# Decoder layer in fp32 on one core: self-attention's v copied by quarters of the rows instead of by copies, with other places for gated transfers and for the closing loads

## The chip, the cores and the metric

The kernel runs on one core of one Trainium2 chip. A core has a matrix engine (TensorE, PE in the profile; PEld is its weight load), a vector engine (DVE), a scalar engine (ACT), GpSimd (POOL) and a queue for transfers (SP). Each takes its instructions in the order of the program and waits for the others through semaphores. SP and ACT both issue DMA transfers: those of SP are queue q1 of the profile, those of ACT are q10. The metric is the device time of one execution in microseconds (us). The kernel before took 848.33, 846.91 and 843.43 us in three runs, median 846.91.

## The reference

One post-norm decoder layer on x (2 x 1024 x 256) with a context of 77 rows per batch entry, all in float32:

```
def _L0_attn_ref(x, Wq, Wk, Wv, Wo, bo):          # 16 heads of 64
    q, k, v = split_heads(x @ Wq), split_heads(x @ Wk), split_heads(x @ Wv)
    q, k = apply_rope(q), apply_rope(k)
    sim = einsum('bid,bjd->bij', q, k) * scale
    sim = where(causal, sim, -inf)
    out = einsum('bij,bjd->bid', softmax(sim), v)
    return merge_heads(out) @ Wo + bo

x = layernorm(x + _L0_attn_ref(x, ...))
x = layernorm(x + _L0_xattn_ref(x, ctx_1024, ...))  # 16 heads over 77 keys
x = layernorm(x + _L0_ffn_ref(x, ...))              # upper half of the rows by w_r through gelu(x W1 + b1) W2 + b2
```

The change is in the first of the three, self-attention, which ends at about 550 us of the 843 us.

## The kernel before

Self-attention works on 16 pairs of heads (2 batch entries x 8), `Pair` n = 0 to 15. Its steps have letters, and the order of all instructions is written out by hand in lists of them: `opening` (L526), a list `steps` (L487) that is run once per period with an offset of pairs for each step, and `ending` (L539). `("V6", -1)` in period p does step V6 of pair p - 1. The order holds for every engine: each gets its part of the list in this order.

The steps of a pair, with the engine that does them:

- `L`: loads its columns of Wk, Wq, Wv (three transfers on SP, w_pair). `Pk`, `Pq`, `Pv`: projections (PE), `E`: their copies out of PSUM (ACT). Digits after them are halves of the 1024 rows.
- `d`: a transfer that swaps neighbouring rows of k and q (turned<-raw, two on SP). `c`, `s`, `a`: the rotation by cosine and sine, on POOL. A half of k and q is ready after its `a`.
- `w` (`spread`, L314): stores v (128 partitions x 1024 numbers) in DRAM as v_d, four quarters of 32 rows. `l` (`copies`, L318): loads v_d back four times into the tile v4, issued by ACT: each group of 32 partitions gets all of v. There is one v4 (`bufs=1`).
- `S0` to `S4`: scores of five groups of query tiles (PE); `T`: mask and row maxima (DVE); `X`: exponentials (ACT); `R`: transposes by 32 x 32 blocks (DVE).
- `V0` to `V7` (`output`, L399): the product of the probabilities with v. Because the transposes are by blocks of 32, the matmuls have 32 rows, and each of the four row groups of PE reads its own copy in v4: matmul (k, j, r) of Vn reads `v4[rows of r, 8k + n, half j]`. These are 488 short matmuls per pair (7808 in all, L410).
- `O`: copies the output out of PSUM (ACT, `gathered`). `Q`, `I`: the row sums turned into a row and inverted; `D`: stores the inverse in DRAM (inv_d); `B` (`along`, L390): loads it back over 64 partitions twice (over<-inv_d, SP). `M` (`scaled`, L430): out times over, on POOL. `W`: stores the pair's result (attn_d).

The closings (`Closing`, L438) make an output tile of 128 rows from all eight pairs: `A` (first batch entry) and `f` (second) load attn_d, `C`/`F` project, `Y`/`g` and `Z`/`z` normalise.

Almost all transfers of SP go through `begin` (L217). It knows a `gate`: after V1 of a pair, `output` puts its last matmul there, and the next transfer that `begin` issues waits for that matmul. What stands behind it on SP waits too.

`pieces` (L228) says for each pair how many extra splits its score and projection matmuls get (`split`), so that the same columns are done in more and smaller instructions.

In the periods in the middle, PE does, from V7 of one pair to V0 of the next: scores, projections for later pairs, scores; then V0 and V1, scores, V2 to V4, scores, V5, V6, V7. `l` for the next pair's V stands behind V7, since v4 is then free.

Of the kernel before, what the change touches and what calls it, by code (L numbers as in the profile page):

```python
# [16 lines left out]
P, R32 = 128, 32  # L17
B, T, C = 2, 1024, 256
# [4 lines left out]
NT = T // P  # L23
# [11 lines left out]
def decoder_layer(  # L35
# [104 lines left out]
    keys = [(b, hp) for b in range(B) for hp in range(NP)]  # L140
# [5 lines left out]
    with (  # L146
# [78 lines left out]

        pieces = [0, 2, 12, 13, 11, 10, 11, 12, 13, 11, 8, 9, 8, 8, 9, 0]  # L228
        left = [pieces[0]]

        def split(first, last, most):
# [14 lines left out]
        class Pair:  # L246
# [71 lines left out]
            def copies(self):  # L318

                self.v4 = s1.tile([P, K4, P], F32, tag="v4", name="v4")  # L320
                for r in range(4):
                    nc.scalar.dma_start(
                        self.v4[r * R32 : (r + 1) * R32, :, :].rearrange("k (c n) d -> k c (n d)", c=4),
                        self.v_d.rearrange("c k e -> k c e"),
                    )


# [71 lines left out]
            def output(self, n):  # L399
                if n == 0:  # L400
                    self.po = [ring.tile([P, NT, R32], F32, tag="t", name="po_self") for _ in range(4)]
                for k in range(4):
                    for j in range(2):
                        first = (NT * n + n, NT * (n + 1) + n)[j]
                        step = (1, NT)[j]
                        last = first + (NT - 1 - n) * step + 1

                        for r in range(k if n == NT - 1 else 0, 4):
                            rows = slice(r * R32, (r + 1) * R32)
                            ins = TE.matmul(  # L410
                                self.po[r][j * D : (j + 1) * D, n:, :],
                                self.v4[rows, NT * k + n, j * D : (j + 1) * D],
                                p_t[rows, first:last:step, k * R32 : (k + 1) * R32],
                                start=(n == 0 and k == 0), stop=(n == NT - 1 and k == r),
                            )
                if n == 1 and self.n < len(keys) - 1:
                    gate[:] = [ins]

            def gathered(self, r):
# [18 lines left out]
        class Closing:  # L438
# [47 lines left out]

        steps = [  # L487
# [40 lines left out]
            0Ev4 0T01 1Pq1 0X00 0c1 0s1 0X01 1Eq1 1Ek1 1Pv0 0a1 0S1 2L 0R00 0w 0R01 1d1 1Pv4 1c1 1Pq0 0T10 0T11  # L528
            0S2 1Ev4 0T21 0X10 1Ev0 1Eq0 1Pk0 1s1 1w 0X11 2Pq1 0T20 0l 0R10 1Ek0 1d0 0S3 0R11 0X21 0X20 0T30
            2Pk0 1a1 0T31 0X30 1c0 0S4 0X31 0R20 1s0 0R30 0R21 1a0 2Eq1 0T40 3L 2Pv4 0T41 2Pv0 0X40 0X41 2Ek0  # L530
            0R31 0R40 2Pq0 2Ev4 5= 1S0 0R41 1T00 2Eq0 2Ev0 0V0 1T01 0V1 2w 0V2 1S1 1T11 0V3 1X00 2d0 0V4 0V5 1T10
            1S2 1X01 1X11 1R00 0V6 0V7 1X10 0O0 1T20 1T21 1S3 1R10 1R01 0O1 2c0 1l 1X20 1T31 2Pk1 0O3 1T30 0O2
            3Pv4 0Q 2Ek1 1S4 2c1 1X30 2s0 1X21 3Pq1 1R20 3Ev4 3Pv0 2a0 1R11 3Pk0 0I 1T41 2d1 1R30 1X31 3Pq0 1T40
            2S0 1R21 1X41 1X40 1R31 1R40 0D 1R41 2T00 3Ek0 2s1 3Eq1 4L 2a1 3Eq0 3Ev0 1V0 1V1 0B 2T01 2X00 1V2 2S1
            1V3 1V4 2T10 2T11 1V5 2R00 2S2 2X01 2T20 2T21 1V6 2X11 2R01 1V7 3d0 3c0
        """


        ending = """  # L539
            14S3 14R11 15s0 14X20 12M 14R20 14X10 14X21 14R10 13O0 14l 13O1 14R21 14T31 15Pk1 15a0 13Q 14T30 13I  # L540
            14S4 14X31 14X30 13O2 14R31 14T41 14X41 14T40 14R30 14R41 4C 12W 13D 15Ek1 15d1 5A 15c1 4Y 13O3 14X40 14R40
            15S0 15s1 15T01 15a1 14V0 15T00 15X01 14V1 13B 14V2 15S1 14V3 14V4 15T10 15T11 15X00 14V5
            15R00 15X11 15S2 14V6 14V7 15X10 15T20 15T21 14O0 15R01 15S3 14O3 5C 15R10 15l 15X21 13M 15T30 15X20
            15T31 15R11 15R21 15X30 15R20 15X31 15R30 14O1 13W 15S4 14Q 15T41 15T40 5U 15R31 14I 14O2 15X41
            15X40 6A 6C 1= 15R40 15R41 15Q 15I 5Y 6U 0f 1f 1= 15V0 14D 4Z 14B 6Y 15V1 15V2 15V3 7A 15V4 5Z 14M 15V5 7C 0n 15V6
            6Z 15D 15B 15V7 15O3 15O0 15O1 2f 15O2 0F 1F 0g 2F 0z 1g 1z 7U 2g 3f 2z 3F 3g 7Y 3z 4f 4F
            4g 7Z 5f 6f 7f 0N 1N 5F 6F 5g 6g 7F 4z 7g 5z 6z 7z
        """
# [569 lines left out]
```

## Time and profile before

| | |
|---|---|
| three runs | 848.33, 846.91, 843.43 us |
| profiled execution | 844.46 us, span 842.7 us |
| mean granted clock of TensorE | 0.983 |
| v<-v_d, issued by ACT | 64 transfers of 512 KB |
| turned<-raw, SP | 64 of 256 KB, 4.3 us from issue to landing (median) |
| v_d<-v, SP | 16 of 512 KB, 4.5 us |
| over<-inv_d, SP | 32 of 256 KB, 4.2 us |
| attn_d<-out_pair, SP | 14 of 512 KB, 3.9 us |
| instruction reads (q8) | 90 packets, 1.47 MB |

The profile is one execution. Its groups of instructions have columns "line, engine, operation, out<-in, form, count | busy us, mean ns of one | idle us of the engine just before them and what ended most of it"; "issue" is idle time in which the engine waited for nothing that the profile shows. A row of the timeline begins with start and length in us. A table by stages has PE, PEld, DVE, ACT and POOL busy times with counts, then the granted clock, the share of the 16 DMA engines' time, and GB/s. Queue rows have packets, MB and the share of 16 DMA engines' span that the packets took. The trace also holds each DMA packet with its queue, size, start and length; a transfer's completion is one packet of 4 bytes from each DMA engine that it used.

### The profile page before, as it was taken

How to read it: one execution, taken by the hardware profiler on the slowest of the kernel's cores; microseconds unless marked ns; L12 is line 12 of the kernel's file. 1: busy time of each engine (PE TensorE's matmuls, PEld its weight loads, DVE VectorE, ACT ScalarE, POOL GpSimd, SP SyncE). 2: the span in 40 equal slices, each digit the busy share in tenths (PEclk: the TensorE clock that was granted, in tenths of full speed). 3: DMA queues.
4: the chain of work that ended last, by engine and by line, in shares of the span. 5: the costliest groups of instructions: out<-in, count | busy, mean ns of one | idle time of the engine just before them, and what ended most of it. 6: DMA issues, size and time to landing. Idle time of an engine off the chain costs nothing.

```text
span 842.7 us, 26522 instructions
## 1 busy us (share of the span) xinstructions
PE 794.6 (94%) x11432; PEld 628.9 (75%) x11432; DVE 575.5 (68%) x1306; ACT 358.2 (43%) x845; POOL 364.4 (43%) x261
## 2 busy tenths in 40 slices
PE   8999999999999999999999999899999999999886
PEld 5566688788788788787788777688778887776645
DVE  2658679668668668678768778345677788866664
ACT  2545456555456555455454455002433333233120
POOL 2633554554454555365463641222133322440473
PEclk9999999999999999999999999899999999999988
DMA  5445377477467577667467476661360000110130
GB/s 187 148 137 140 108 203 199 155 192 203 123 174 193 161 209 197 170 174 188 143 167 190 140 177 174 174 215 44 102 240 1 1 1 1 42 60 1 51 112 38
DMA packets 65329, 112.32 MB, mean 133 GB/s; under 512 B 6498, under 2 KB 43708, under 8 KB 65212
## 3 DMA queue, kind: packets, MB, share of 16 engines
q1 hardware_dynamic: 54459, 72.87, 26.8%
q10 hardware_dynamic: 9216, 33.56, 18.3%
q0 software_dynamic: 1536, 4.20, 1.3%
q8 instruction: 90, 1.47, 0.7%
q14 instruction: 28, 0.22, 0.1%
HBM read 71.24 MB, written 22.59 MB: 111 GB/s over the span
## 4 chain that ended last, share of the span: by engine, by line
PE 84%; DVE 9%; issue 4%; POOL 1%; ACT 1%; DMA 0%; POOLq 0%; SPq 0%; DVEq 0%; ACTq 0%
PE po_self L410 18%; PE ps_scores L342 16%; PE pp_kq L268 13%; PE pp_v L303 7%; PE ps_cross L934 6%; PE po_cross L977 6%; PE po_proj L473 5%; PE po_ffn L886 3%; PE pp_h L875 3%; DVE reach L800 2%; DVE pT L372 2%; PE unread L244 1%; DVE p L355 1%; PE pt_p L965 1%; DVE e L943 1%
## 5 line engine op out<-in xcount | busy, mean ns | idle before, releaser
L355 DVE CUSTOM_DVE_ANT_0 p<-ps_scores,fence 128x512 f32<-128x512 f32 (+7 forms) x256 | 179.7, 751 | 124.1 <-PE ps_scores L342 123.6
L363 ACT ACTIVATE p<-p,neg 128x768 f32<-128x768 f32 (+7 forms) x256 | 196.3, 768 | 160.2 <-DVE neg L355 158.3
L410 PE MATMUL po_self<-pT,v 32*64 32x256 f32 (+6 forms) x7808 | 160.5, 300 | 22.2 <-issue 18.6
L372 DVE STREAM_TRANSPOSE pT<-p 128x768 f32<-128x768 f32 (+7 forms) x256 | 175.7, 740 | 4.1 <-ACT p L363 2.5
L410 PEld LDWEIGHTS po_self<-pT,v 32*64 32x64 f32 x7808 | 139.6, 134 | 47.1 <-issue 35.0
L342 PE MATMUL ps_scores<-kq 64*128 64x256 f32 (+3 forms) x1056 | 150.6, 417 | 1.8 <-issue 1.5
L342 PEld LDWEIGHTS ps_scores<-kq 64*128 64x128 f32 x1056 | 94.4, 189 | 43.5 <-issue 29.9
L268 PE MATMUL pp_kq<-xT,w_pair 128*128 128x256 f32 (+2 forms) x516 | 118.8, 383 | 0.8 <-ACT xT L203 0.8
L288 POOL TENSOR_TENSOR kq<-raw,cos 128x1024 f32<-128x1024 f32 x31 | 73.2, 2362 | 105.9 <-ACT raw L276 105.9
L291 POOL TENSOR_TENSOR turned<-turned,sin 128x1024 f32<-128x1024 f32 x31 | 73.2, 2362 | 103.2 <-DMA turned<-raw 103.2
L268 PEld LDWEIGHTS pp_kq<-xT,w_pair 128*128 128x128 f32 x516 | 87.2, 191 | 24.7 <-issue 11.6
L955 POOL TENSOR_TENSOR e<-e,inv 128x616 f32<-128x616 f32 x32 | 38.2, 1217 | 116.6 <-DVE inv L954 83.4
L120 POOL TENSOR_TENSOR rs<-ve,neg_half 128x1 f32<-128x1 f32 x48 | 27.4, 576 | 116.4 <-DVE ve L118 114.2
L295 POOL TENSOR_TENSOR kq<-kq,turned 128x1024 f32<-128x1024 f32 x31 | 73.5, 2370 | 1.4
L977 PE MATMUL po_cross<-packed,pT 128*128 128x256 f32 (+1 forms) x320 | 71.8, 379 | 0.1
L934 PE MATMUL ps_cross<-wqk,x1T 128*128 128x308 f32 x256 | 69.3, 424 | 1.4 <-ACT x1T L924 1.4
L977 PEld LDWEIGHTS po_cross<-packed,pT 128*128 128x128 f32 (+1 forms) x320 | 60.8, 190 | 10.2 <-issue 0.5
L303 PEld LDWEIGHTS pp_v<-w_pair,xT 128*128 128x128 f32 x512 | 61.1, 192 | 4.0 <-issue 2.2
L303 PE MATMUL pp_v<-w_pair,xT 128*128 128x128 f32 x512 | 62.2, 275 | 0.0
L934 PEld LDWEIGHTS ps_cross<-wqk,x1T 128*128 128x128 f32 x256 | 47.4, 190 | 17.9 <-ACT x1T L924 1.7
L947 ACT ACTIVATE e<-e 128x616 f32<-128x616 f32 x32 | 22.9, 717 | 76.7 <-DVE e L943 75.4
L473 PE MATMUL po_proj<-wo,attnT 128*128 128x256 f32 x224 | 51.7, 383 | 0.5 <-DVE out_pair L428 0.5
(123 smaller groups left out, 816.8 us busy)
## 6 DMA issues: line engine op xcount, KB each, us to landing
v<-v_d ACTq DMA_DIRECT2D x64, 512.0 KB, 8.3
turned<-raw SPq DMA_DIRECT2D x64, 256.0 KB, 4.3
v_d<-v SPq DMA_DIRECT2D x16, 512.0 KB, 4.5
over<-inv_d SPq DMA_DIRECT2D x32, 256.0 KB, 4.2
attn_d<-out_pair SPq DMA_DIRECT2D x14, 512.0 KB, 3.9
attnT<-attn_d SPq DMA_DIRECT2D x8, 512.0 KB, 5.5
vo_d<-vo SPq DMA_DIRECT2D x2, 1232.0 KB
attnT<-attn_d SPq DMA_DIRECT2D x3, 768.0 KB, 5.4
```

The source lines that it names most:

```text
L268: TE.matmul(pp[:, cols], self.w[:, c, "kq".index(of), :], x_ts[self.b, n][:, c, cols], start=(c == 0), stop=(c == NC - 1),)
L288: E.tensor_tensor(self.kq[:, :, n * NB : (n + 1) * NB], self.raw[n], self.twice(cos, n), ALU.mult)
L295: E.tensor_tensor(dst, dst, self.turned[n], ALU.add)
L303: TE.matmul(pv[:, i, :], x_ts[self.b, 2 * n // NT][:, c, toks], self.w[:, c, 2, :], start=(c == 0), stop=(c == NC - 1),)
L342: TE.matmul(self.ps[j][:, cols], self.kq[rows, 1, t * P : (t + 1) * P], self.kq[rows, 0, cols.start - at : cols.stop - at], start=True, st ...
L355: V.tensor_tensor_reduce(p[:, span], self.ps[j][:, span], fence[:, T - (t + 1) * P :], -SCALE, -MASKED, ALU.add, ALU.min, neg[:, i : i + 1],)
L363: A.activation(p[:, span], p[:, span], AF.Exp, bias=neg[:, i : i + 1], scale=-1.0, accum_out=self.sums[:, j, t : t + 1],)
L372: V.transpose(p_t[:, first : first + t * step + 1 : step, :], self.p[g, j][:, span].rearrange("p (n k) -> p n k", k=P),)
L410: ins = TE.matmul(self.po[r][j * D : (j + 1) * D, n:, :], self.v4[rows, NT * k + n, j * D : (j + 1) * D], p_t[rows, first:last:step, k * R ...
L473: TE.matmul(self.po, of, wo[:, c, :], start=(c == 0), stop=(c == NP - 1))
L934: TE.matmul(ps[:, g, : Q * S], self.x_t[:, c, :], wqk[:, c, self.b, h : h + Q, :].rearrange("p h s -> p (h s)"), start=(c == 0), stop=(c = ...
L977: TE.matmul(po, self.p_t[:w, k, :], packed[self.b][:w, k, :], start=(k == 0), stop=(k == NK - 1))
```

## The change

It has four parts.

1. **copies.** Four transfers of 512 KB remain. Each brought all of v to one group of 32 partitions; now each brings one quarter of the rows (32 rows of 4 KB) to all four groups, 128 partitions, by a source that repeats the quarter four times.
2. **Gates and places.** `output` sets the gate after V6 as well as after V1. `w` moves from between V1 and V2 to behind V6, and `B` from the same place to behind `w` (in the opening: 2w behind 0V6, 0B behind 1V6; there d of the next pair takes the gate of V1).
3. **pieces.** Five of the sixteen entries grow by one; their sum goes from 137 to 142.
4. **Ending.** The load 5A moves from before V0 of pair 14 to behind its V1, 13B from behind V1 to behind V6 of pair 14, 6A from before V0 of pair 15 to behind 13B, and 0f and 1f from before V0 of pair 15 to behind its V3 and the load 7A.

```
-        pieces = [0, 2, 12, 13, 11, 10, 11, 12, 13, 11, 8, 9, 8, 8, 9, 0]
+        pieces = [0, 2, 13, 13, 12, 10, 11, 13, 13, 12, 8, 9, 8, 9, 9, 0]
...
-                for r in range(4):
+                for c in range(4):
                     nc.scalar.dma_start(
-                        self.v4[r * R32 : (r + 1) * R32, :, :].rearrange("k (c n) d -> k c (n d)", c=4),
-                        self.v_d.rearrange("c k e -> k c e"),
+                        self.v4[:, c * NT : (c + 1) * NT, :].rearrange("p n d -> p (n d)"),
+                        self.v_d[c].unsqueeze(0).to_broadcast([4, R32, NT * P]),
                     )
...
-                if n == 1 and self.n < len(keys) - 1:
+                if n in (1, NT - 2) and self.n < len(keys) - 1:
                     gate[:] = [ins]
...
-            ("T00", 0), ("T01", 0), ("s1", 0), ("V0", -1), ("a1", 0), ("V1", -1), ("d0", 1), ("B", -2), ("w", 1), ("S1", 0), ("V2", -1),
+            ("T00", 0), ("T01", 0), ("s1", 0), ("V0", -1), ("a1", 0), ("V1", -1), ("d0", 1), ("S1", 0), ("V2", -1),
...
-            ("V6", -1), ("T21", 0), ("V7", -1), ("X10", 0), ("X20", 0), ("O1", -1), ("S3", 0),
+            ("V6", -1), ("w", 1), ("B", -2), ("T21", 0), ("V7", -1), ("X10", 0), ("X20", 0), ("O1", -1), ("S3", 0),
...
-            14S4 14X31 14X30 13O2 14R31 14T41 14X41 14T40 14R30 14R41 4C 12W 13D 15Ek1 15d1 5A 15c1 4Y 13O3 14X40 14R40
-            15S0 15s1 15T01 15a1 14V0 15T00 15X01 14V1 13B 14V2 15S1 14V3 14V4 15T10 15T11 15X00 14V5
-            15R00 15X11 15S2 14V6 14V7 15X10 15T20 15T21 14O0 15R01 15S3 14O3 5C 15R10 15l 15X21 13M 15T30 15X20
+            14S4 14X31 14X30 13O2 14R31 14T41 14X41 14T40 14R30 14R41 4C 12W 13D 15Ek1 15d1 15c1 4Y 13O3 14X40 14R40
+            15S0 15s1 15T01 15a1 14V0 15T00 15X01 14V1 5A 14V2 15S1 14V3 14V4 15T10 15T11 15X00 14V5
+            15R00 15X11 15S2 14V6 13B 6A 14V7 15X10 15T20 15T21 14O0 15R01 15S3 14O3 5C 15R10 15l 15X21 13M 15T30 15X20
...
-            15X40 6A 6C 1= 15R40 15R41 15Q 15I 5Y 6U 0f 1f 1= 15V0 14D 4Z 14B 6Y 15V1 15V2 15V3 7A 15V4 5Z 14M 15V5 7C 0n 15V6
+            15X40 6C 1= 15R40 15R41 15Q 15I 5Y 6U 1= 15V0 14D 4Z 14B 6Y 15V1 15V2 15V3 7A 0f 1f 15V4 5Z 14M 15V5 7C 0n 15V6
```

More of the change, by code (lines that the diff above doesn't have):

```diff
@@ L530, in decoder_layer @@
             2Pk0 1a1 0T31 0X30 1c0 0S4 0X31 0R20 1s0 0R30 0R21 1a0 2Eq1 0T40 3L 2Pv4 0T41 2Pv0 0X40 0X41 2Ek0
-            0R31 0R40 2Pq0 2Ev4 5= 1S0 0R41 1T00 2Eq0 2Ev0 0V0 1T01 0V1 2w 0V2 1S1 1T11 0V3 1X00 2d0 0V4 0V5 1T10
-            1S2 1X01 1X11 1R00 0V6 0V7 1X10 0O0 1T20 1T21 1S3 1R10 1R01 0O1 2c0 1l 1X20 1T31 2Pk1 0O3 1T30 0O2
+            0R31 0R40 2Pq0 2Ev4 5= 1S0 0R41 1T00 2Eq0 2Ev0 0V0 1T01 0V1 2d0 0V2 1S1 1T11 0V3 1X00 0V4 0V5 1T10
+            1S2 1X01 1X11 1R00 0V6 2w 0V7 1X10 0O0 1T20 1T21 1S3 1R10 1R01 0O1 2c0 1l 1X20 1T31 2Pk1 0O3 1T30 0O2
             3Pv4 0Q 2Ek1 1S4 2c1 1X30 2s0 1X21 3Pq1 1R20 3Ev4 3Pv0 2a0 1R11 3Pk0 0I 1T41 2d1 1R30 1X31 3Pq0 1T40
-            2S0 1R21 1X41 1X40 1R31 1R40 0D 1R41 2T00 3Ek0 2s1 3Eq1 4L 2a1 3Eq0 3Ev0 1V0 1V1 0B 2T01 2X00 1V2 2S1
-            1V3 1V4 2T10 2T11 1V5 2R00 2S2 2X01 2T20 2T21 1V6 2X11 2R01 1V7 3d0 3c0
+            2S0 1R21 1X41 1X40 1R31 1R40 0D 1R41 2T00 3Ek0 2s1 3Eq1 4L 2a1 3Eq0 3Ev0 1V0 1V1 3d0 2T01 2X00 1V2 2S1
+            1V3 1V4 2T10 2T11 1V5 2R00 2S2 2X01 2T20 2T21 1V6 0B 2X11 2R01 1V7 3c0
         """
```

## The prediction

> **What bounds the kernel now.** I read the page first: engines, then the queues, then the costliest groups.
>
> ```profile
> span 842.7 us, 26522 instructions
> PE 794.6 (94%) x11432; PEld 628.9 (75%) x11432; DVE 575.5 (68%) x1306; ACT 358.2 (43%) x845; POOL 364.4 (43%) x261
> q1 hardware_dynamic: 54459, 72.87, 26.8%
> q10 hardware_dynamic: 9216, 33.56, 18.3%
> ...
> L410 PE MATMUL po_self<-pT,v 32*64 32x256 f32 (+6 forms) x7808 | 160.5, 300 | 22.2 <-issue 18.6
> ...
> v<-v_d ACTq DMA_DIRECT2D x64, 512.0 KB, 8.3
> ```
>
> TensorE is busy for 94%, so only a new PE wait or a removed one moves the end. The removable one stands in the L410 row: 22.2 us of idle time before the output matmuls, nearly all "issue". The profile's own time is 844.46 us, 1.8 above its span and 2.45 below the median 846.91; I sum against 844.46.
>
> v's copies are all of queue q10 (ACT issues nothing else). To see where they lie I took one pair's stretch in the timeline, the waits on v_d, and the busy table from the copies' issue to V0 of the next pair:
>
> ```profile
> 259.86 0.31 ACTq L322 DMA_DIRECT2D v<-v_d  x1
> ...
> 260.48 1.27 ACTq L322 DMA_DIRECT2D v<-v_d  x3
> ...
> 275.98 3.50 PE L410 MATMUL po_self<-pT,v 32*64 32x256 f32 x128
> ...
> 289.13 1.08 PE L410 MATMUL po_self<-pT,v 32*64 32x64 f32 x82 [1.70 <-issue]
> ```
>
> ```profile
>   PEld po_self L410: 0.5, 1
> ```
>
> ```profile
> 259.80:276.00 16.20, 16.20 (x128) 14.41 (x128) 11.84 (x17) 9.75 (x20) 6.52 (x3) 1.00 0.95 242
> ```
>
> The copies can start only when V7 has read the single v4 buffer, and V0 of the next pair reads all of it: 16.1 us for 2 MB. The packet records show the first copy packet at 261.1 and the last completion at 272.2, so 3.8 us are spare; in all pairs together PE waits 0.5 us for them. But the window's DMA share is 0.95: it is already full with the copies spread over all 16 engines. **Whatever makes the copies longer by more than 4 us stops PE once per pair.**
>
> **The copies (the part that decides).** Bytes stay: four transfers of 128 rows of 4 KB per pair. Before, each transfer's source and destination both begin with a dimension of 32 (32x4x1024); after, the destination begins with 128 partitions, and the source with the broadcast: 4 copies of stride 0, then 32 rows.
>
> First the row. q10 has 9216 packets = 64 transfers x (128 data + 16 completions): each one used 16 engines. 18.3% of 16 x 842.7 us is 2467 us over 8192 data packets, 0.30 us each; the records give 0.159 for the median 4 KB packet of q1. A transfer of 32 rows at a time puts two engines on each way into the memory, which fits the doubling and the Trainium skill ("SBUF — State Buffer", section "Door 1: The DMA port swizzle"): 32 neighbouring partitions reach 8 of 16 ports, partition p shares one with p+32. By this rule alone the change halves the packet: 32 packets per engine x 0.159 = 5.1 us instead of 9.6, no cost.
>
> Against it speaks "DMA: Bandwidth & Descriptors", section "Why a DMA increments its semaphore by 16 and not by 1" and its rules for authors: the number of engines is the largest up to 16 that divides the slowest dimension of both sides, and a leading zero-stride broadcast of c copies confines the transfer to c engines, on hardware queues the lowest-numbered ones. The trace bears the dividing out: q1 holds 4961 packets of 4 bytes; 1152 are data (b_r, b1), which leaves 3809 completions for 239 transfers = 236 x 16 + 3 x 11, and exactly three transfers have 77 partitions, whose largest divisor is 11. No transfer of the trace begins with a 4. I take 4 engines, and the same 4 for all copies. Then each of them moves 4 x 128 / 4 = 128 rows per pair:
> - lower end, 0.159 us a packet, nothing beside it: 20.4 us; with 0.7 to the completion B = 21.1.
> - upper end, 0.30 as in q10's row: 38.4 us; d1, w_pair and attn_d, some 1.4 MB in this stretch, add 86 KB per engine, 3.3 us at 26 GB/s (4 KB in 0.159): B = 42.4.
> - taken: 0.21. Copy r goes to partitions 32r to 32r+31, so engines 0 and 1 (2 and 3) walk over the same ports in step, four rows to a port. In the trace's burst the first three packets of each engine still took 0.159 before they doubled; two or three fast ones of four give (2.5 x 0.159 + 1.5 x 0.30) / 4 = 0.21. B = 26.9 + 3.3 + 0.7 = 30.9.
>
> From first copy packet to V0 the 15 later pairs have 13.4 to 19.1 us, 243.4 in sum (pair 0 has 21.3). PE's new wait: 15 x 30.9 - 243.4 = 220, plus 9.6 for pair 0: **+230 us**. At the ends: +73 and 15 x 42.4 - 243.4 + 21 = +414.
>
> **TensorE's clock.** The records of the granted clock show 0.5 for 3.4 us at single places of this stage (at 227 and 531 us, for two), behind gaps of PE. Each new wait of some 15 us will bring one: 3.4 us of work at half speed lose 1.7, x 15 = **+26** (lower end +10, upper +40). PEclk will show it.
>
> **ACT's issue.** Transfers with a broadcast source (over<-inv_d, SP) cost 0.55 us apiece against the copies' 0.40: +0.6 us per pair on an engine that is 43% busy, followed by the last two gathers. Hidden; if not, at most 15 x 0.6 = 9 us.
>
> **w and B behind V6, w gated.** SP then holds v_d<-v until V6's last matmul, about 259.2 (the group at 258.30 is V6 and V7) instead of 252.3, and over twice behind it, about 260 instead of 250.5. Behind them on SP stands d1 (265.4 us): nothing late. v_d is copied one period later: hidden. over is waited for by M on POOL, and behind M in POOL's order stand c1 (265.40), a0 (267.73 to 270.10), and S0 on PE at 274.25. At 4.2 us to land M starts at about 265, c1 about 2 us late, of a0's 4.15 us of slack half is left: nothing. Beyond 267.1 every microsecond is one for S0; with 4 engines the V0 behind it waits anyway and takes that up.
> The gain meant here is V2 to V7 without transfers beside PE's instruction reads (queue q8, 90 packets, 1 us each). Bounds: 0, since those reads do not take longer when transfers run (0.88 to 1.66 us, without order), and -22, the whole L410 idle. I take -8, some 0.6 of the 1.2 to 1.9 us of "issue" before V6 in each of 13 pairs.
>
> **Pieces and PE's waits.** Five more splits are ten more matmul calls, under 1 us. A first matmul that needs one copy instead of four saves 47 wait instructions on PE, 51 ns each: -2 at most. Together -1. That V0's first quarter needs only the first copy gains nothing: its fourth needs the last.
>
> **Ending.** Loads 5A, 6A, 0f, 1f and B of pair 13 change places on SP; 0f goes from before 15V0 (528.7) to behind 7A (some 540) and takes 5.4 us; first used at 550.2. Hidden by 4 us; if 7A waits longer, up to +5. 0 taken.
>
> **Sum**: 844.5 + 230 + 26 - 8 - 1 = **1092 us**; its own range 844.5 + 73 + 10 - 22 = 905 to 844.5 + 414 + 40 = 1299.
>
> **The rivals.**
> 1. *Four engines, 1092 us, chance 0.80.* For it: the divisor seen in the trace's 11s, and a window with DMA share 0.95. Against: no broadcast of 4 in the trace.
> 2. *All 16 engines (or the four transfers on four different sets) and all ports: faster.* The burst falls from 11 to about 6 us, nothing waits for it, and the quiet V2 to V7 gives back half of 22: 844.5 - 11 = **833.5**. It decides as soon as one copy's completion comes from 16 engines. Chance 0.10.
> 3. *16 engines, but nothing was on the path:* the copies were waited for 0.5 us in all, instruction reads do not shorten: **844**. Chance 0.05.
> 4. *16 engines, B too late:* turned<-raw beside today's burst took 8.1 us to land; over, issued at 260.5, then lands at 268.6, 1.5 us after M's limit of 267.1, and S0 waits that long in 13 pairs: 844.5 + 20 = **864**. Chance 0.05, since the burst would be shorter.
>
> **How the numbers follow.** What the measurement can tell from no change is about 0.5%, 4 us. Slower: 0.80 + 0.05 = 0.85; faster 0.10; within 0.05. The range that holds 8 in 10 takes all of case 1 but its last tail, and case 4: 860 to 1290.
>
> **What would show it.** q10's packets: 8192 + 64 x 4 = 8448 instead of 9216 shows the engines; their share times 16 times the span, over 8192, tells 0.159 from 0.30 us a packet. A new row po_self waiting for DMA v<-v_d with some 15 us in each of 15 pairs, median landing above 15 us instead of 8.3, V0 to V0 about 45 us instead of 31. "issue" before L410 falling under 15 shows the gate. I am wrong if q10 still has 9216 packets, or if the copies' burst stays under 15 us.

## The result and the profile after

The changed kernel takes 1055.24 us (median of four runs, 1053.73 to 1056.99) against 845.17 us of the kernel before beside it: a ratio of 1.250, 95% interval 1.244 to 1.256. The profiled execution took 1053.73 us, its span is 1052.0 us, and TensorE's mean granted clock fell from 0.983 to 0.899.

First the page of the changed kernel: engines, the granted clock by slices, the two queues, the chain that ended last by engine, and three groups of instructions.

```profile
span 1052.0 us, 26531 instructions
PE 844.0 (80%) x11452; PEld 644.3 (61%) x11452; DVE 573.7 (55%) x1306; ACT 354.0 (34%) x845; POOL 363.5 (35%) x261
...
PEclk9989879698898989879898988987999999999989
...
q1 hardware_dynamic: 54459, 72.87, 22.1%
q10 hardware_dynamic: 8448, 33.56, 9.3%
...
DMA 45%; PE 41%; DVE 5%; issue 3%; ACTq 3%; ACT 2%; POOL 1%; POOLq 0%; DVEq 0%; SPq 0%
...
L410 PE MATMUL po_self<-pT,v 32*64 32x256 f32 (+6 forms) x7808 | 195.9, 338 | 134.6 <-DMA v<-v_d 128.7
...
L342 PE MATMUL ps_scores<-kq 64*128 64x256 f32 (+3 forms) x1076 | 157.5, 430 | 19.4 <-POOL kq L295 19.4
...
L431 POOL TENSOR_TENSOR out_pair<-out_pair,over 128x1024 f32<-128x1024 f32 x15 | 35.5, 2367 | 157.0 <-DMA over<-inv_d 143.9
```

In the kernel before the chain was PE's, and neither the scores (L342) nor M (L431) waited to speak of. Its chain, its group L342 and its waits of M (us in total, times, longest):

```profile
PE 84%; DVE 9%; issue 4%; POOL 1%; ACT 1%; DMA 0%; POOLq 0%; SPq 0%; DVEq 0%; ACTq 0%
...
L342 PE MATMUL ps_scores<-kq 64*128 64x256 f32 (+3 forms) x1056 | 150.6, 417 | 1.8 <-issue 1.5
...
POOL out_pair L431 <- DMA over<-inv_d: 8.3, 3, 4.1
```

q10 moves the same 33.56 MB in 8448 packets: 8192 of data and 256 completions, four for each of 64 transfers. **Each copy used 4 engines instead of 16.** Its share, 9.3% of 16 x 1052 us, makes 1565 us, or 0.19 us per data packet (0.190 in the packet records; the median packet took 0.159 instead of 0.322) against 0.30 before: the packets did get faster, but four engines do the work of sixteen. Bytes and packets of q1 are unchanged.

The waits of PE, longest sums first (us in total, times, longest):

```profile
PE po_self L410 <- DMA v<-v_d: 128.7, 30, 6.0
PE ps_scores L342 <- POOL kq L295: 19.4, 7, 4.1
PE po_proj L473 <- DMA attnT<-attn_d: 12.2, 1, 12.2
```

The span grew by 209.3 us. PE's busy time took 49.4 of them (794.6 to 844.0), nearly all in self-attention (50 to 550 us before, 50 to 757 after) at a granted clock of 0.86 instead of 0.98; its idle time took 160, of which the waits on v_d went from 0.5 to 128.7, and "issue" before L410 from 18.6 to 2.1. The stage by the tables, before and after:

```profile
50.00:550.00 500.00, 475.39 (x9884) 386.82 (x9882) 356.20 (x774) 256.90 (x630) 246.46 (x119) 0.98 0.63 169
...
50.00:757.00 707.00, 523.25 (x9797) 400.19 (x9796) 355.30 (x774) 253.71 (x631) 246.98 (x119) 0.86 0.38 121
```

One pair's timeline shows how a period now runs (start, length; in square brackets the idle time before it and what ended it):

```profile
438.18 0.52 ACTq L322 DMA_DIRECT2D v<-v_d  x1
438.25 2.03 SPq L219 DMA_DIRECT2D over<-inv_d  x2
...
438.73 7.51 ACTq L322 DMA_DIRECT2D v<-v_d  x3
...
446.29 0.37 ACT L422 COPY out_pair<-po_self 128x256 f32<-128x256 f32 x1 [7.59 <-issue]
...
450.03 2.37 POOL L431 TENSOR_TENSOR out_pair<-out_pair,over 128x1024 f32<-128x1024 f32 x1 [15.38 <-DMA over<-inv_d]
...
457.08 3.28 PE L342 MATMUL ps_scores<-kq 64*128 64x256 f32 x20 [4.06 <-POOL kq L295]
...
460.29 1.12 PE L410 MATMUL po_self<-pT,v 32*64 32x256 f32 x32
...
464.29 1.16 PE L410 MATMUL po_self<-pT,v 32*64 32x256 f32 x16 [2.88 <-DMA v<-v_d]
...
470.99 3.36 PE L410 MATMUL po_self<-pT,v 32*64 32x256 f32 x71 [5.54 <-DMA v<-v_d]
```

The chain of waits through the same stretch has one long piece:

```profile
440.16 30.78 DMA v<-v_d
```

From the issue of the copies (438.2) to V0's last quarter (470.99) are 32.8 us. In the pair that the prediction shows, V0 as a whole began 16.1 us after the issue (259.86 to 275.98). PE is not idle all that time: the work beside the copies is slower, S0 is late, and V0 runs in pieces as quarters land. So the rows of single waits understate the cause.

A cleaner reading is by the copies themselves. The packet records give, for each pair, the **burst** (first to last packet of q10) and the **gap** from its end to the next pair's first packet; 15 of each fill the time from the end of pair 0's burst to the end of the last pair's. "beside" is what q1 moved during a burst, on average of pairs 2 to 13. The kernels below the first two are experiments:

| kernel | burst, mean | 15 bursts | gap, mean | 15 gaps | beside, MB |
|---|---|---|---|---|---|
| before | 11.4 | 171 | 20.8 | 311 | 0.36 |
| after | 29.1 | 436 | 16.1 | 241 | 1.99 |
| e2_copies | 26.7 | 400 | 17.7 | 266 | 1.46 |
| e10_afterB | 26.5 | 397 | 16.4 | 246 | 1.46 |
| e6_busy9 | 27.7 | 415 | 16.3 | 245 | 1.77 |
| e1_rest | 14.2 | 212 | 21.1 | 316 | 1.24 |
| e9_Bback | 11.6 | 174 | 20.1 | 301 | 0.44 |
| e3_rows | 7.8 | 117 | 28.7 | 431 | 0.27 |

Before, part of each gap was spare time of the copies. After, the last quarter of the next V0 starts 0.4 to 0.5 us after the burst's end, and a period is burst plus gap: bursts and gaps together went from 482 to 678 us, pair 0's burst added 16.6 us, and these 212 us are the whole loss (the stretch behind the last burst became 3.6 us shorter, the one ahead of the first 0.8 longer).

### The profile page after: what moved, and what is told of

Same layout as the page of the kernel before. It is cut to its first block, busy times and chain, and to the rows that moved or that the text cites. A ratio compares the mean times of both kernels' runs of the same rounds, so it can differ in the third digit from the quotient of the medians.

```text
span 1052.0 us, 26531 instructions
## 1 busy us (share of the span) xinstructions
PE 844.0 (80%) x11452; PEld 644.3 (61%) x11452; DVE 573.7 (55%) x1306; ACT 354.0 (34%) x845; POOL 363.5 (35%) x261
## 3 DMA queue, kind: packets, MB, share of 16 engines
q1 hardware_dynamic: 54459, 72.87, 22.1%
q10 hardware_dynamic: 8448, 33.56, 9.3%
## 4 chain that ended last, share of the span: by engine, by line
DMA 45%; PE 41%; DVE 5%; issue 3%; ACTq 3%; ACT 2%; POOL 1%; POOLq 0%; DVEq 0%; SPq 0%
DMA v<-v_d 45%; PE po_self L410 13%; PE ps_scores L342 5%; PE ps_cross L934 5%; PE po_cross L977 5%; PE po_proj L473 3%; PE po_ffn L886 3%; ACTq L322 3%; PE pp_h L875 2%; DVE reach L800 1%; PE pp_kq L268 1%; PE pt_p L965 1%; DVE e L943 1%; PE ps_vo L741 1%; ACT p L363 1%
## 5 line engine op out<-in xcount | busy, mean ns | idle before, releaser
L410 PE MATMUL po_self<-pT,v 32*64 32x256 f32 (+6 forms) x7808 | 195.9, 338 | 134.6 <-DMA v<-v_d 128.7
L410 PEld LDWEIGHTS po_self<-pT,v 32*64 32x64 f32 x7808 | 146.1, 147 | 186.7 <-DMA v<-v_d 147.0
L342 PE MATMUL ps_scores<-kq 64*128 64x256 f32 (+3 forms) x1076 | 157.5, 430 | 19.4 <-POOL kq L295 19.4
L342 PEld LDWEIGHTS ps_scores<-kq 64*128 64x128 f32 x1076 | 101.2, 202 | 63.5 <-issue 30.4
L268 PE MATMUL pp_kq<-xT,w_pair 128*128 128x256 f32 (+2 forms) x516 | 119.4, 383 | 3.7 <-ACT raw L276 1.7
L268 PEld LDWEIGHTS pp_kq<-xT,w_pair 128*128 128x128 f32 x516 | 86.7, 191 | 28.8 <-issue 13.2
L431 POOL TENSOR_TENSOR out_pair<-out_pair,over 128x1024 f32<-128x1024 f32 x15 | 35.5, 2367 | 157.0 <-DMA over<-inv_d 143.9
L303 PEld LDWEIGHTS pp_v<-w_pair,xT 128*128 128x128 f32 x512 | 61.4, 194 | 9.5 <-ACT out_pair L422 5.7
L303 PE MATMUL pp_v<-w_pair,xT 128*128 128x128 f32 x512 | 63.4, 279 | 4.1 <-ACT out_pair L422 4.1
L473 PE MATMUL po_proj<-wo,attnT 128*128 128x256 f32 x224 | 53.2, 391 | 12.7 <-DMA attnT<-attn_d 12.2
```

The costliest lines, as they stand in the source:

```text
L268: TE.matmul(pp[:, cols], self.w[:, c, "kq".index(of), :], x_ts[self.b, n][:, c, cols], start=(c == 0), stop=(c == NC - 1),)
L303: TE.matmul(pv[:, i, :], x_ts[self.b, 2 * n // NT][:, c, toks], self.w[:, c, 2, :], start=(c == 0), stop=(c == NC - 1),)
L342: TE.matmul(self.ps[j][:, cols], self.kq[rows, 1, t * P : (t + 1) * P], self.kq[rows, 0, cols.start - at : cols.stop - at], start=True, st ...
L410: ins = TE.matmul(self.po[r][j * D : (j + 1) * D, n:, :], self.v4[rows, NT * k + n, j * D : (j + 1) * D], p_t[rows, first:last:step, k * R ...
L473: TE.matmul(self.po, of, wo[:, c, :], start=(c == 0), stop=(c == NP - 1))
```

## The experiments

Times are medians; the kernel before took 842.4 to 843.2 us beside them.

**1. The places without the copies (e1_rest).** The change with the copies of before:

```
-                for c in range(4):
+                for r in range(4):
                     nc.scalar.dma_start(
-                        self.v4[:, c * NT : (c + 1) * NT, :].rearrange("p n d -> p (n d)"),
-                        self.v_d[c].unsqueeze(0).to_broadcast([4, R32, NT * P]),
+                        self.v4[r * R32 : (r + 1) * R32, :, :].rearrange("k (c n) d -> k c (n d)", c=4),
+                        self.v_d.rearrange("c k e -> k c e"),
```

> The changed kernel with the copies of before (32 partitions at a time), all other parts of the change kept. Theory (the copies run on four engines, and that is the whole loss): 9216 packets on q10, PE waits for v<-v_d under 5 us in all, time within 1% of before, 837 to 853 us, 845 taken. Rival 1 (the places of w and B and the second gate cost by themselves, since M and S0 come late): 860 to 900 us with ps_scores waiting for kq on POOL. Rival 2 (they gain on instruction reads, as the prediction took with -8): under 840 us and 'issue' before the L410 matmuls below 12 us.

Measured: 895.74 us, ratio 1.062 (1.058 to 1.066). I had not foreseen this size: the places cost some 53 us by themselves, as the first rival had it. Its page, groups of L342, L410 and M, and the median landing of over (last figure, us):

```profile
L342 PE MATMUL ps_scores<-kq 64*128 64x256 f32 (+3 forms) x1076 | 163.7, 436 | 47.3 <-POOL kq L295 43.5
...
L410 PE MATMUL po_self<-pT,v 32*64 32x256 f32 (+6 forms) x7808 | 160.2, 303 | 5.7 <-issue 5.6
...
L431 POOL TENSOR_TENSOR out_pair<-out_pair,over 128x1024 f32<-128x1024 f32 x15 | 35.4, 2362 | 173.4 <-DMA over<-inv_d 173.4
...
over<-inv_d SPq DMA_DIRECT2D x32, 256.0 KB, 7.8
```

M waits for over, which lands in 7.8 us instead of 4.2: it is now issued just ahead of the copies and runs beside them (1.24 MB beside a burst instead of 0.36). c and a of the next pair stand behind M on POOL, S0 behind a. "issue" before L410 fell from 18.6 to 5.6: V2 to V7 did become quieter.

**2. The copies alone (e2_copies).** The kernel before with the changed copies only (the same lines, the other way round).

> Before with the copies of the change alone. Theory: 8448 packets on q10, PE waits 110 to 150 us for v<-v_d, time 1040 to 1070 us, as the whole change. Rival 1 (places and gates share the loss): 950 to 1030 us.

Measured: 1041.92 us, ratio 1.235 (1.230 to 1.240), q10 again 8448 packets. With experiment 1, 199 + 53 is more than the 210 of the whole: the parts overlap or help each other. Experiments 9 and 10 take that apart.

**3. All 16 engines and all rows distinct (e3_rows).** The kernel before, with v stored four times in DRAM, so that a copy reads 128 separate rows:

```
-                    self.v_d = dram.tile([4, R32, NT * P], F32, tag="v", name="v_d")
+                    self.v_d = dram.tile([4, 4, R32, NT * P], F32, tag="v", name="v_d")
...
-                begin(self.v_d.rearrange("r k e -> (r k) e"), self.v.rearrange("p n d -> p (n d)"))
+                for c in range(4):
+                    begin(
+                        self.v_d[c].rearrange("r k e -> k r e"),
+                        self.v[c * R32 : (c + 1) * R32].rearrange("p n d -> p (n d)").unsqueeze(1).to_broadcast([R32, 4, NT * P]),
+                    )
...
-                for r in range(4):
+                for c in range(4):
...
+                        self.v4[:, c * NT : (c + 1) * NT, :].rearrange("p n d -> p (n d)"),
+                        self.v_d[c].rearrange("r k e -> (r k) e"),
```

> Before, with each quarter of v stored four times in DRAM (four stores of 32 partitions with a repeated source instead of one of 128), so that a copy reads 128 different rows for 128 partitions and has no broadcast; the same 512 KB per copy. Theory (number of engines from the slowest dimension of both sides, and 16 ways into the memory when 128 partitions are written): 9216 packets on q10, 0.16 to 0.19 us each instead of 0.30, burst of one pair's copies 5.5 to 7.5 us instead of 11, time 838 to 855 us since PE did not wait for the copies before either. Rival (writing 128 partitions by quarters is itself slow, whatever the source): burst over 20 us and time over 1000 us.

Measured: 914.09 us, ratio 1.086 (1.081 to 1.091). Queues, and the output matmuls (L414 here, L410 in the other kernels):

```profile
q1 hardware_dynamic: 61371, 98.03, 36.7%
q10 hardware_dynamic: 9216, 33.56, 10.4%
...
L414 PE MATMUL po_self<-pT,v 32*64 32x256 f32 (+6 forms) x7808 | 162.1, 300 | 55.8 <-issue 52.6
```

9216 packets are 16 engines per copy again, the destination of each is the same 128 partitions as in the change, and the burst is 7.8 us, shorter than before's 11.4; a packet takes 0.185 us. So it is the repeated source that takes the engines away, and with separate rows this destination gives the short burst that rival 2 hoped for. The time was missed all the same. The stores, 98.03 - 72.87 = 25 MB more, run beside V1 to V6. PE's idle time grew by 44 us, 42 of them "issue" (18.6 to 52.6 before the output matmuls, 7.9 before L268), and its busy time by 24.5 (794.6 to 819.1) at a clock of 0.956 instead of 0.983. The gaps grew by 120 us, of which 54 only stand in for the shorter bursts.

**4. and 6. TensorE kept busy before V0 (e4_busy, e6_busy9).** The whole change, with matmuls whose results nobody reads before V0 of pairs 2 to 14: fill(24), 48 instructions, in experiment 4, and fill(9), 18 instructions of 8.0 to 9.4 us together, in experiment 6, whose edit this is.

```
+                    if 1 < self.n < len(keys) - 1:
+                        fill(9)
```

> The changed kernel with 24 unread matmuls of 128x512 (some 10 us) on PE before V0 of pairs 2 to 14, where it otherwise waits for the copies; they add work and leave nothing out. Theory (49 us of the 209 are TensorE's clock at half speed after each wait): mean granted clock of 0.96 or more instead of 0.90, the time falls to 1005 to 1030 us. Rival (PE's longer busy time is not the clock's, or the clock falls anyway): 1050 to 1065 us.

> The changed kernel with 9 unread matmuls of 128x512 before V0 of pairs 2 to 14 (18 instructions of 0.44 us, 7.9 us, inside the wait of 8.6 us per pair; the 24 of the earlier run were 21 us and longer than the wait); they add work only. Theory (the clock's half speed behind each wait is part of the loss, some 45 us): mean granted clock 0.94 or more, time 1010 to 1035 us. Rival (the filling delays the work behind it as much as the clock gives back): 1045 to 1075 us.

Measured: 1168.88 us and 1035.80 us (ratio 1.234, 1.227 to 1.242). In experiment 4 the filling, some 21 us, was longer than the wait, so it tells only that the clock follows: 0.976. In experiment 6 the clock rose from 0.899 to 0.96:

```profile
PEclk9999889999999989999999999897899999999989
...
L412 PE MATMUL po_self<-pT,v 32*64 32x256 f32 (+6 forms) x7808 | 172.7, 312 | 57.5 <-DMA v<-v_d 40.2
```

19 us came back, and by the table they lie in the bursts (436 to 415), not in the gaps (241 to 245). The shorter bursts are those where over came earlier: in pairs 4, 5, 6, 11 and 12 its transfers were issued some 4 us before the burst instead of 2, 1.4 to 1.7 MB ran beside it instead of 2.0, and it took 25.6 to 27.0 us instead of 28.8 to 29.9. In the gaps two things cancel: from V0's last quarter to the next copies PE's busy time fell from 15.6 to 14.6 us a pair, and its idle time grew from 0.1 to 1.2, most of it "issue" (17.3 us in all before the output matmuls, 2.1 in the change). So the run says little of what the half clock costs.

**5. Two engines (e5_two).** If the number of repeats sets the engines, two repeats must leave two. The kernel before with copies as eight transfers of 64 partitions:

```
+                for c in range(4):
+                    for h in range(2):
+                        nc.scalar.dma_start(
+                            self.v4[h * 2 * R32 : (h + 1) * 2 * R32, c * NT : (c + 1) * NT, :].rearrange("p n d -> p (n d)"),
+                            self.v_d[c].unsqueeze(0).to_broadcast([2, R32, NT * P]),
```

> Before with the copies for two groups of partitions at a time: eight transfers of 64 partitions (256 KB) per pair instead of four, the source a quarter of v repeated twice; bytes unchanged. Theory (a leading dimension of 2 leaves two engines): q10 has 8192 + 128 x 2 = 8448 packets, no more than two of them at any time, burst 256 x 0.19 + 3 to 5 = 52 to 54 us per pair, time 845 + 16 x 53 - 265 + clock 50 = some 1450 to 1520 us. Rival (the copies of the change lost by something else than engines, the repeated reads of one row say): with half the repeats per transfer the time falls, 940 to 1040 us.

Measured: 1368.31 us, a single run. The count of engines holds, the time was put too high:

```profile
span 1366.5 us, 26557 instructions
...
q10 hardware_dynamic: 8448, 33.56, 6.5%
```

8448 is now 8192 + 128 transfers x 2. The burst is 47.4 us: 256 packets on each engine at the 0.159 us of an undisturbed packet are 40.7, so 6.7 are left for the 1.46 MB of other traffic beside it.

**7. and 8. w and gate without B (e7_w, e8_wB).** The kernel before with the gate after V6 and w behind V6, B where it was; in experiment 8, B is moved the other way, ahead of V0.

```
-                if n == 1 and self.n < len(keys) - 1:
+                if n in (1, NT - 2) and self.n < len(keys) - 1:
...
+            ("V6", -1), ("w", 1), ("T21", 0), ("V7", -1), ("X10", 0), ("X20", 0), ("O1", -1), ("S3", 0),
```

> Before with the second gate and w behind V6, as in the change; B stays behind V1, copies, pieces and ending as before. Theory (of the 52 us that places and gates cost alone, B behind V6 is the cause, since over lands late for M; w there is free and V2 to V6 have less traffic beside the instruction reads): 832 to 846 us, PE waits under 5 us for kq of POOL, 'issue' before the L410 matmuls 8 to 18 us. Rival (w or the gate itself costs): 860 to 890 us.

> The same with B moved before V0 instead, so that only d0 moves data between V1 and V6. Theory (over lands before M, and the 'issue' waits before L410 shrink as in the run of places and gates, to 4 to 10 us): 826 to 840 us. Rival (over beside V0 and V1 stops those instead, or B waits on SP for the inverse and holds d0): 846 to 870 us.

Measured: 838.35 us, ratio 0.997 (0.994 to 0.999), and 846.79 us, ratio 1.006 (1.004 to 1.009). Experiment 7's groups:

```profile
L410 PE MATMUL po_self<-pT,v 32*64 32x256 f32 (+6 forms) x7808 | 157.8, 297 | 10.3 <-issue 8.1
...
L342 PE MATMUL ps_scores<-kq 64*128 64x256 f32 (+3 forms) x1056 | 148.1, 412 | 3.1 <-POOL kq L295 2.5
```

w and the gate take 10.5 us of "issue" from L410, but only about 3 us from the time. Experiment 7 is the fastest version found; its gain is at the limit of what can be measured. B ahead of V0 more than gives it back, as the rival had it ("issue" 13.4 there); by which of the rival's two ways was not traced.

**9. and 10. Only B put back (e9_Bback, e10_afterB).** Experiment 1 and the whole change, each with B between V1 and V2 again (13B behind 14V1 in the ending, 0B behind 1V1 in the opening):

```
-            ("T00", 0), ("T01", 0), ("s1", 0), ("V0", -1), ("a1", 0), ("V1", -1), ("d0", 1), ("S1", 0), ("V2", -1),
+            ("T00", 0), ("T01", 0), ("s1", 0), ("V0", -1), ("a1", 0), ("V1", -1), ("d0", 1), ("B", -2), ("S1", 0), ("V2", -1),
...
-            ("V6", -1), ("w", 1), ("B", -2), ("T21", 0), ("V7", -1), ("X10", 0), ("X20", 0), ("O1", -1), ("S3", 0),
+            ("V6", -1), ("w", 1), ("T21", 0), ("V7", -1), ("X10", 0), ("X20", 0), ("O1", -1), ("S3", 0),
```

> The change with the copies of before (as in the first experiment, 895.7 us) and only B put back between V1 and V2. If B behind V6 is the whole of those 52 us: 836 to 846 us, PE's idle time before L342 under 6 us (47.3 there), no M waiting for over<-inv_d. If the pieces or the closings carry part of it: above 855 us.

> The whole change, with its copies, and only B put back between V1 and V2. If the copies alone set the period and B's lateness lies beside their wait: 1038 to 1055 us, the rows of PE waiting for DMA v<-v_d growing by what the rows L342 waiting for POOL kq lose. If the two costs add up as they do in their own runs: about 1005 us.

Measured: 842.71 us (ratio 1.000, 0.997 to 1.002) and 1020.31 us (ratio 1.212, 1.205 to 1.218). The first says that B was the whole of experiment 1's loss (before L342 6.1 us are left of 47.3, 1.9 of them for kq); w, pieces and closings cost nothing to be seen. The second fell between its two expectations. Its groups:

```profile
L410 PE MATMUL po_self<-pT,v 32*64 32x256 f32 (+6 forms) x7808 | 199.8, 338 | 143.9 <-DMA v<-v_d 136.7
...
L342 PE MATMUL ps_scores<-kq 64*128 64x256 f32 (+3 forms) x1076 | 150.7, 415 | 0.0
```

Putting B back takes away PE's waits for kq (19.4) and attnT (12.2) and gives 8.0 back as waits for v_d, but the table names the carrier: bursts of 26.5 instead of 29.1 us, 397 against 436 in sum, with over's two transfers, 0.52 MB, no longer among the copies. That is 39 of bursts less 5 of gaps, 34 us, the difference of the two spans (33.6).

So the 210 us are, from the medians: places without B 0, **the copies on four engines +177** (1020.3 - 842.7, both with B in its old place), **B in the copies' way +35** (1055.2 - 1020.3). And w with its gate, worth about 3 us to the kernel before, is worth 22 with the slow copies (experiment 2 against 10, which differ in the pieces and closings too).

## Why the prediction was right, and where its sum was off

The likeliest case, four engines, is what happened, and the 1055 us lie in its own range; the sum's 1092 is 37 too high. By its steps:

- **Four engines: right.** The signs named for it are there: 8448 packets, a period of 45 us instead of 32, "issue" before L410 under 15. The rule that the Trainium skill gives in "DMA: Bandwidth & Descriptors", section "Why a DMA increments its semaphore by 16 and not by 1", agrees with both points measured here: four repeats, four completions; two repeats, two. The sign "some 15 us of waiting in each pair" did not show: V0 waits in pieces, two a pair on average, 8.6 us together.
- **The burst: right in size, wrong in its parts.** 30.9 us were forecast, 29.1 measured. A packet was put at 0.21 and took 0.190, and its excess over 0.159, which is still its median, goes with other traffic: 128 x 0.159 = 20.4 leaves 6.1 us for 1.46 MB beside the burst (experiment 10) and 8.7 for 1.99 MB (the change), over 4 us per MB, where the sum had 3.3 us for 1.4 MB. The rise from 0.159 to 0.21 I had put down to engines walking over the same ports; these numbers need no such term. Two errors of about equal size cancelled, which is luck.
- **PE's wait of +230: right in kind, 44 too high; here the sum was off.** The prediction counted the room for the copies up to V0's start, and put at nothing that V0 can begin with the first of them. But in the pair shown two quarters of V0 ran at 460.29, the third at 464.29, and only the fourth waited for the last landing. The kernel before started that last quarter 1.4 us after V0's start: from the first copy packet to it the 15 pairs had 264.2 us, not 243.4. (To V0's very first matmul the records even give 238.8, because the last pair starts with a few matmuls at 11.3 us and then waits for DVE.) After the change they have 442.1, and pair 0 went from 22.6 to 30.4: 178 + 8 = +186. Of the 44 us too many, 22 are the three early quarters, and 22 the burst, whose 30.9 stands against 29.5 from first packet to last quarter.
- **The clock, +26 on top: about right.** From V0's last quarter to the next copies nothing covers slower work. One such stretch and the sum of all 15, before and after:

```profile
277.33:291.63 14.30, 12.60 (x478) 9.89 (x464) 10.30 (x30) 7.66 (x25) 8.69 (x4) 1.00 0.35 113
...
sum 211.65, PE 193.42 PEld 152.75 DVE 149.84 ACT 110.36 POOL 97.39; mean PE 12.89 PEld 10.18 DVE 9.99 ACT 7.36 POOL 6.49
...
470.99:486.35 15.36, 15.27 (x480) 11.60 (x481) 9.68 (x23) 4.89 (x13) 3.05 (x2) 0.91 0.30 105
...
sum 235.55, PE 233.37 PEld 178.52 DVE 134.37 ACT 69.53 POOL 33.37; mean PE 15.56 PEld 11.90 DVE 8.96 ACT 4.64 POOL 2.22
```

  The 15 stretches grew by 24 us, from 14.1 to 15.7 each. The mean clock in them fell from 0.989 to 0.875, which by the clock's records is 27 us more of lost work; that is the larger part of the 40 us by which PE's busy time grew there, while its idle time fell by 16. The records show half clock for longer than the 3.4 us of the prediction (11 of 26 stretches have 10.2), but these begin in the waits: of 463.6 to 473.8 in the pair shown, 2.8 us lie behind the start of V0's last quarter. Experiments 9 and 10, which differ in the copies alone, say the same: 14.1 us at clock 1.00, 16.0 at 0.87. PE's busy time grew by 49 in all, twice what I took, because half clock also lies beside the bursts (0.85 there), where the copies cover it. No run changes the clock and nothing else.
- **w and B behind V6 at nothing: wrong for B, +35.** The prediction priced over by when it lands, and let V0's wait take the delay up. It missed that over shares the four engines and the time of the copies and makes every burst 2.6 us longer. Rival 4 had the mechanism without slow copies at 20 us; experiment 1 shows 53: over lands in 7.8 us beside the copies of before, and M's lateness passes on to S0 in 13 pairs, 43.5 us of waits.
- **Instruction gaps, -8: inside its bounds.** "issue" before L410 fell by 10.5 without the slow copies, worth 3 us, and with them the difference was near the upper bound of 22 (experiments 2 and 10).
- **ACT's issue "hidden": held for the end, not for ACT.** ACT was blocked for 7.5 us in the pair shown, which the prediction had at 0.6 more than before. PE's waits behind ACT's gathers make 12 us (4.1 before L303, 3.7 before L380, 3.2 before L202, 1.2 before L268), more than the 9 allowed, but all lie beside bursts.
- **Pieces and ending: right.** Experiment 9 shows no cost. The 12.2 us before po_proj are gone with B put back (experiment 10), though a wait of 7.7 us stands there in experiment 7 too, where B of pair 13 is in its old place; they lay beside the last burst, and the stretch behind it did not grow.

In sum: 186 up to V0's last quarter, 24 from there to the next copies, and the rest within 1 us make the 209.3 of the span, against 230 and 26 - 8 - 1. Inside the 186 are the 39 us by which B makes the bursts longer, which the sum did not have: without B the bursts are 26.5 us, 4.4 under the forecast. That the total came within 37 us is in part luck.

## What to carry to other kernels

Before a transfer is made wider, count the engines it will use: the completions in the packet records tell them for each shape, and a repeated source put outermost left as many as it has repeats. Where a transfer fills its queue's whole share of a period, add up periods by its burst and the gap to the next one; single waits and a slower clock beside the burst are already in it, a slower clock in the gap is not hidden by it. Count the wait from the work that needs the last part of the transfer; work that can run on the first parts lies in its cover. What else is put beside such a burst lengthens it, even if nobody waits for that other transfer.

## What the runs showed of the hardware that was not expected

- **Issue blocks the engine.** With the copies on four engines the longest issue of a copy on ACT took 6.9 us (1.8 before, median 0.62 against 0.44), and in the kernel with two engines, where the longest took 7.1 us, ACT stood idle for up to 27.7 us ("issue") before its gathers, 323.5 us in all.
- **Instruction gaps end behind an instruction read.** PE's "issue" before the output matmuls was 18.6 us before, 8.1 with v's store moved out of V2 to V6, and 52.6 with 25 MB more stored there. Each of these gaps of over 0.8 us (11 before, 5 in experiment 7, 22 in experiment 3) ended 1.2 to 1.6 us after the end of a packet of q8. The gaps grew with the traffic; the reads themselves took no longer at the median (1.06, 1.14 and 0.96 us). What makes them late is not shown, and other things move the gaps too: 2.1 us in the change, 17.3 with 18 more matmuls a pair (experiment 6).
- **Packets got faster with the wider destination.** The same 4 KB packets took 0.300 us each when a transfer went to 32 partitions, and 0.185 when it went to 128, both on 16 engines. The sources differ too (experiment 3 reads separate rows, the kernel before one set of rows four times), and no run changes the destination alone.
